# A gate input fetched three steps ahead, first in its step, with three buffers; eleven buffers for z instead of twelve

## The chip, the cores and the metric

The kernel runs on one core of one Trainium2 chip. The metric is device time in microseconds (us) of one execution, given as the median of several runs. A profiled execution is a separate one: its trace has a start and an end for each instruction of the five engines (TensorE = PE, with its weight loads shown apart as PEld; VectorE = DVE; ScalarE = ACT; GpSimd = POOL; SyncE = SP). SP does no arithmetic here. It issues nearly all transfers between the device's memory and the on-chip buffers.

## The reference, cut to what matters

Two equal layers are applied to an image x of 512 x 512 places with 64 channels. In each, x is normalised by groups of two channels over the whole image (`_gn`) and then by channels at each place (`_ln`); five products with 64 x 128 weights follow; `left` and `right` are gated; a band of nine rows of `left` is multiplied into `right`; the result is normalised over its 128 channels, multiplied by an output gate and projected back to 64 channels.

```python
xn = _ln(x, norm_scale, norm_bias)
left = (xn @ Wl + bl) * mask * jax.nn.sigmoid(xn @ Wlg + blg)
right = (xn @ Wr + br) * mask * jax.nn.sigmoid(xn @ Wrg + brg)
out_gate = jax.nn.sigmoid(xn @ Wog + bog)
out = _banded_ingoing(left, right, WIN)
out = _ln(out, out_norm_scale, out_norm_bias) * out_gate
return out @ Wo + bo
...
x = x + _L0_conv_ref(_gn(x), L0_conv_src_mask, L0_conv_norm_scale, ...)
x = x + _L1_conv_ref(_gn(x), L1_conv_src_mask, L1_conv_norm_scale, ...)
```

## The kernel before

Each layer goes over nine blocks of 64 rows (`row_blocks`), and each block in two chunks of 16 steps, so a layer has 18 chunks and 288 units of work. A unit is 64 rows by 8 columns in each half of the image (`Unit`); what leaves the layer is made in units too (`Out`). `layer` (line 784) first plans at which step each part of the work of each unit falls, and then runs a loop over steps `t` (line 846). In one step parts of several units are in hand:

- the input `z` of a unit far ahead is loaded (`load`, two transfers of 128 KB). It is scaled and moved (POOL), its statistics are taken (DVE), and one step before the unit's own step it is transposed on PE (`transposed`) and copied to `zT` by ACT (`kept`). The transposes are the last readers of the `z` buffer. `zp` (line 388) has twelve buffers. The plan lets the load run 9 to 12 steps ahead of the unit's own step, and in most of the steps of a chunk it loads one unit, in some two or none;
- `kept` also stores `zT`, the transposed input, to the device's memory under the name `later` (line 483, 256 KB), because the output gate needs it 17 or 33 steps on. `zT` has two buffers, so the copy of one unit waits for the store of the unit two before;
- `right` (line 516) is the projection of the unit from `zT`, 32 small matrix products, in two halves, "project 0" and "project 4"; ACT makes the sigmoid `sg`, and DVE the product `RO`;
- `take_left` (line 561) loads a slab `A` of the band, four transfers of 128 KB each. A chunk needs eight slabs, so they fall into a part of the steps only; `mix` ("band") multiplies with it;
- for an output unit `o`, `recall` (line 686) loads the stored `zT` back into `zg` (256 KB, pool `ztg`, line 1067, two buffers). `gates` (line 690) multiplies it with the gate's weights, in four matrix products, the only readers of `zg`; `gated` is the sigmoid of that on ACT (`gate`); `turned`, `times_gate` (DVE, `ZH`) and `end` follow; `ended` adds the residual `XR`, which `fetch` (line 739) loaded by two transfers, and stores two transfers to `mid_x` (layer 0) or to the output (layer 1).

The order of the instructions on every engine is the program's own: `InOrder` (line 373) holds each engine to the order in which the program issues, and that is why most of the profile's lines are L381, the line of that helper. Within a step the items run in the order of the lists `FIRST` and `SECOND` (lines 38 and 47). "gates" stands ahead of the projections in both, "transpose" and "keep" in the second half of the list, "end" after them in `FIRST` and just after "keep" in `SECOND`.

SP's queue in a step before the change is: loads of `z` (lines 849 to 851), two of `XR` for the next step, the slabs `A`, the load of `zg` for the step after the next (lines 856 and 857), and then, as the items come, the store of `zT` and the two stores of the output unit before. Each transfer can wait on a semaphore ahead of its issue, and what is behind it in the queue waits with it. The pools' buffers come free at run time: a load into a used buffer waits for the last reader of what was there. The load of `zg` in step `t` waits so for the gate products of step `t` itself, as there are two buffers and it loads for step `t + 2`.

Of the kernel before, what the change touches and what calls it, by code (L numbers as in the profile page):

```python
# [103 lines left out]
def tile_two_banded_layers(  # L104
# [280 lines left out]
            InOrder, (nc.tensor, nc.vector, nc.scalar, nc.gpsimd, nc.sync)  # L385
        )

    zp = ctx.enter_context(tc.tile_pool(name="zp", bufs=12))

    class Unit:  # L390

# [7 lines left out]
    def load(src: bass.AP, u: Unit):  # L399
        u.z = zp.tile([P, JU, D], F32, tag="z", name="z")  # L400
        if u.near is None:
            rows = slice(u.blk.s, u.blk.s + S)
            for e, j in enumerate((u.j, LH + u.j)):
                en.sync.dma_start(u.z[e * S : (e + 1) * S], src[rows, j : j + JU, :])
            return
        spans = [(0, u.near, u.near + JU)]
        if u.near + JU > NEAR * JQ:
            spans = [(o, u.near, u.near + JQ) for o in range(0, JU, JQ)]
        for o0, n0, n1 in spans:
            for o, r, k, m in runs(n0, n1):  # L410
                z = u.z[:, o0 + o : o0 + o + m, :].rearrange("q m c -> q (m c)")
                at, q0, q1 = r * (L + 1) + k - WIN, 0, P
                pieces = []

                if r == 0 and k < WIN:
                    q0, g = 1, min(m, WIN - k)
                    pieces = [(0, 0, g, 0), (0, g, m, at + g)]
                if r == JQ - 1 and k + m > WIN + 1:
                    q1, g = P - 1, max(0, WIN + 1 - k)
                    end = (P - 1) * JQ * (L + 1) + at  # L420
                    pieces = [(P - 1, 0, g, end), (P - 1, g, m, L * L - m)]
                en.sync.dma_start(
                    z[q0:q1],
                    strided(
                        src, (q0 * JQ * (L + 1) + at) * D, (JQ * (L + 1) * D, q1 - q0), (1, m * D)
                    ),
                )
                for q, g0, g1, a in pieces:
                    if g0 < g1:
                        en.sync.dma_start(  # L430
                            z[q : q + 1, g0 * D : g1 * D],
                            strided(src, a * D, (D, 1), (1, (g1 - g0) * D)),
                        )
# [127 lines left out]
    def take_left(n: int, h: int) -> bass.AP:  # L561


        A = lp.tile([P, HA // 2, S, 2], F32, tag="A", name="A")
        q = HA // 4
        for e in range(2):
            for s in range(2):
                en.sync.dma_start(
                    A[e * S : (e + 1) * S, s * q : (s + 1) * q].rearrange("p h i t -> p h (i t)"),
                    strided(  # L570
                        left_of, n * size + (s * H // 4 + h * q) * span + 2 * WIN,
                        (H // 2 * span, S), (span, q), (1, 2 * S),
                    ),
                )
        return A
# [110 lines left out]
    def recall(o: Out):  # L686
        o.t = ztg.tile([P, JU // 2, P], F32, tag="zg", name="zg")
        en.sync.dma_start(o.t, later[o.at])
# [95 lines left out]
    def layer(src: bass.AP, dst: bass.AP, w: dict, stats: bool, then=None):  # L784
# [4 lines left out]
        units, outs, lefts, mixes, looks, slabs = {}, {}, {}, {}, {}, {}  # L789
# [4 lines left out]
        for c in range(n_chunks):  # L794
            b, t0 = blocks[c // per], (c + 1) * NU
            for k in range(NU):
                t = c * NU + k
# [18 lines left out]
        for n in range(0, NEAR * JQ, JU):  # L816
            t = 3 + n // JU * 2
# [28 lines left out]
        for t in range(min(loads), last_t + 3):  # L846
            if then and t == max(units) + 2:
                then()
            for u in loads.get(t, []):
                if u not in early:  # L850
                    load(src, u)
            if t + 1 in outs:
                fetch(src, outs[t + 1], w, t + 1)
            for c, h in slabs.get(t, []):
                A[c, h] = take_left(c // per, h)
            if t + 2 in outs:
                recall(outs[t + 2])

            looking = []
            for o, k in looks.get(t, []):  # L860
# [26 lines left out]
            for item in order:  # L887
                name, n = item if isinstance(item, tuple) else (item, None)
# [120 lines left out]


    two = layer(mid_x, out, w, False)
    one = layer(x, mid_x, w, True, lambda: next(two))
    with tc.tile_pool(name="setup", bufs=1) as tmp:

# [49 lines left out]
    later = dram.tile([len(blocks) * LH // JU, P, JU // 2, P], F32, name="later")  # L1064

    ztp = ctx.enter_context(tc.tile_pool(name="ztp", bufs=2))
    ztg = ctx.enter_context(tc.tile_pool(name="ztg", bufs=2))
    lp = ctx.enter_context(tc.tile_pool(name="lp", bufs=NA))
    wk = ctx.enter_context(tc.tile_pool(name="wk", bufs=3))
    onp = ctx.enter_context(tc.tile_pool(name="onp", bufs=1))  # L1070
# [14 lines left out]
def build(arrays):  # L1085
    import concourse.bacc as _bacc

    nc = _bacc.Bacc("TRN2", target_bir_lowering=False, num_devices=1)
    aps = {}
    for name in _INS:  # L1090
        a = arrays[f"in_{name}_dram"]
        aps[name] = nc.dram_tensor(
            f"in_{name}_dram", a.shape, mybir.dt.from_np(a.dtype), kind="ExternalInput"
        ).ap()
    out = nc.dram_tensor("out_0_dram", aps["x"].shape, F32, kind="ExternalOutput").ap()
    layers = [{n: aps[f"L{i}_conv_{n}"] for n in _NAMES} for i in range(2)]
    with tile.TileContext(nc) as tc:  # L1097
        tile_two_banded_layers(tc, aps["x"], layers, out)
    return nc
# [10 lines left out]
```

## Time and profile before

| what | value |
|---|---|
| median of three runs | 4771.6 us (4764.16 to 4789.46) |
| the profiled execution, its time | 4769.15 us |
| the profiled execution, span from first to last instruction | 4767.2 us |
| busy share of the span: PE, PEld | 81%, 70% |
| busy share: DVE, ACT, POOL | 84%, 76%, 69% |
| mean granted TensorE clock over the span | 0.952 |
| bytes moved, mean rate | 983.48 MB, 206 GB/s |
| share of the 16 transfer engines taken by SP's queue (q1) | 74.4% |
| loads of `zg` | 576 of 256 KB |

The shares are means over stages that are unlike one another. The first 480 us or so are statistics and set-up, the first layer's output steps run from about 510 to 2540 us, the second layer's from about 2790 to 4760. An idle stretch of an engine is put down to the semaphore that ended it. "Busy" for PE means that a matrix product was in the array by a model of its end, and a busy SP is not shown at all, since all that SP does here is to wait and to issue.

### The profile page before, as it was taken

How to read it: one execution, taken by the hardware profiler on the slowest of the kernel's cores; microseconds unless marked ns; L12 is line 12 of the kernel's file. 1: busy time of each engine (PE TensorE's matmuls, PEld its weight loads, DVE VectorE, ACT ScalarE, POOL GpSimd, SP SyncE). 2: the span in 40 equal slices, each digit the busy share in tenths (PEclk: the TensorE clock that was granted, in tenths of full speed). 3: DMA queues.
4: the chain of work that ended last, by engine and by line, in shares of the span. 5: the costliest groups of instructions: out<-in, count | busy, mean ns of one | idle time of the engine just before them, and what ended most of it. 6: DMA issues, size and time to landing. Idle time of an engine off the chain costs nothing. (4 is left out here: it accounts for less than half of the span.)

```text
span 4767.2 us, 193179 instructions
## 1 busy us (share of the span) xinstructions
PE 3885.2 (81%) x76306; PEld 3337.2 (70%) x76306; DVE 4007.1 (84%) x10943; ACT 3608.6 (76%) x8410; POOL 3274.7 (69%) x3427
## 2 busy tenths in 40 slices
PE   1035899999999999999985478888888888888898
PEld 0024787888787878887864467777777777777776
DVE  7864888888888888888877488988899998999898
ACT  0023888888888888898974378888888888888887
POOL 0036888888888888888723487777777777777751
PEclk9987999999999999999997799999999999999999
DMA  7958677777777777777764867777777777777776
GB/s 311 401 120 126 182 208 204 212 217 211 212 208 208 210 208 209 214 212 210 207 171 110 104 189 208 214 220 208 210 221 214 221 212 211 213 219 215 217 200 185
DMA packets 1437809, 983.48 MB, mean 206 GB/s; under 512 B 167363, under 2 KB 1284585, under 8 KB 1432553
## 3 DMA queue, kind: packets, MB, share of 16 engines
q1 hardware_dynamic: 1432064, 969.69, 74.4%
q8 instruction: 604, 9.90, 0.9%
q14 instruction: 301, 2.46, 0.2%
q10 hardware_dynamic: 4840, 1.43, 0.1%
HBM read 658.35 MB, written 312.40 MB: 204 GB/s over the span
## 5 line engine op out<-in xcount | busy, mean ns | idle before, releaser
L381 ACT ACTIVATE on<-RO,nm,rs 128x128 f32<-128x128 f32 x3744 | 1588.5, 492 | 91.8 <-DVE nm L381 44.9
L381 PEld LDWEIGHTS banks<-pack,zT 64*128 64x128 f32 x18576 | 1304.4, 203 | 380.6 <-ACT zT L381 204.4
L381 PE MATMUL banks<-pack,zT 64*128 64x128 f32 x18576 | 1350.8, 292 | 174.4 <-ACT zT L381 149.3
L381 DVE TENSOR_TENSOR RO<-banks,sg 128x512 f32<-128x512 f32 (+1 forms) x1188 | 796.3, 677 | 464.4 <-ACT sg L381 387.6
L381 POOL TENSOR_SCALAR on<-RO,rs,nm 128x128 f32<-128x128 f32 x864 | 383.9, 451 | 975.7 <-ACT sg L381 504.5
L381 ACT ACTIVATE sg<-banks 128x512 f32<-128x512 f32 (+1 forms) x1188 | 695.0, 590 | 311.1 <-PE banks L381 287.1
L381 PE MATMUL bank<-zg,pack 64*128 64x448 f32 (+1 forms) x2304 | 727.3, 615 | 213.5 <-DMA zg<-later 193.8
L381 DVE BATCH_NORM_STATS2 sto<-RO 128x6 f32<-128x256 f32 x2304 | 803.8, 412 | 0.8
L381 DVE SCALAR_TENSOR_TENSOR ZH<-bank,pack,gate 128x448 f32<-128x448 f32 (+1 forms) x1152 | 739.5, 684 | 63.0 <-ACT gate L381 34.1
L381 ACT ACTIVATE gate<-bank 128x448 f32<-128x448 f32 (+1 forms) x1152 | 563.8, 541 | 172.6 <-issue 103.0
L381 POOL TENSOR_TENSOR z<-z,ga 128x512 f32<-128x512 f32 x536 | 681.2, 1279 | 17.2 <-DMA z<-mid_x 8.7
L381 PE MATMUL bank<-pack,ZH 128*64 128x64 f32 x18432 | 667.3, 226 | 17.8 <-DVE nm L381 16.7
L381 POOL TENSOR_TENSOR z<-z,gb 128x512 f32<-128x512 f32 x536 | 677.5, 1277 | 5.1
L381 POOL TENSOR_TENSOR z<-z,rs 128x512 f32<-128x512 f32 x586 | 618.3, 1056 | 71.6 <-DVE rs L381 44.6
L381 POOL TENSOR_TENSOR z<-z,sti 128x512 f32<-128x512 f32 x586 | 624.3, 1066 | 20.8 <-DVE sti L381 20.8
L381 PEld LDWEIGHTS bank<-pack,ZH 128*64 128x64 f32 x18432 | 587.4, 138 | 60.9 <-DVE nm L381 24.2
L381 ACT ACTIVATE zT<-banks 128x512 f32<-128x512 f32 (+1 forms) x1084 | 460.1, 475 | 72.0 <-PE banks L381 62.8
L381 DVE BATCH_NORM_STATS2 sti<-z 128x6 f32<-128x128 f32 x2344 | 504.1, 282 | 0.5 <-POOL z L381 0.3
L381 PE MATMUL bank<-ident,on 64*128 64x64 f32 x9216 | 453.8, 227 | 27.5 <-ACT gate L381 25.0
L381 PEld LDWEIGHTS bank<-zg,pack 64*128 64x128 f32 x2304 | 240.5, 191 | 336.5 <-DMA zg<-later 62.7
L381 PEld LDWEIGHTS bank<-ident,on 64*128 64x128 f32 x9216 | 426.5, 141 | 69.6 <-ACT gate L381 44.7
L381 DVE TENSOR_TENSOR XR<-bank,XR 120x512 f32<-120x512 f32 (+1 forms) x576 | 390.9, 679 | 2.5 <-PE bank L381 1.2
(154 smaller groups left out, 4020.5 us busy)
## 6 DMA issues: line engine op xcount, KB each, us to landing
later<-zT SPq DMA_DIRECT2D x576, 256.0 KB
A<-left_of SPq DMA_DIRECT2D x1152, 128.0 KB
zg<-later SPq DMA_DIRECT2D x576, 256.0 KB
z<-in_x_dram SPq DMA_DIRECT2D x576, 128.0 KB
z<-mid_x SPq DMA_DIRECT2D x576, 128.0 KB
gn_x<-in_x_dram SPq DMA_DIRECT2D x16, 4096.0 KB
XR<-in_x_dram SPq DMA_DIRECT2D x448, 112.0 KB
mid_x<-XR SPq DMA_DIRECT2D x448, 112.0 KB
```

The lines of the kernel that those rows point to most:

```text
L381: return lambda *a, **k: tc.keep_in_program_order(f(*a, **k))
```

## The change

It edits four places. `zp` has eleven buffers instead of twelve, `ztg` three instead of two; both tiles take the same room, so what is in the on-chip memory stays the same in sum. The load of `zg` in step `t` is for the output unit of step `t + 3` instead of `t + 2`, and it is issued ahead of the step's loads of `z`, `XR` and `A` instead of behind them. No transfer is added, none is removed, and the order of the instructions on PE, DVE, ACT and POOL is the same as before; on SP only the places of the `zg` loads differ. With three buffers the load in step `t` again waits for the gate products of step `t`. In the steps in which the plan loads 12 steps ahead (four of a chunk's sixteen), the load of `z` with eleven buffers waits for the transposes of the very step in which it stands; with twelve it waits for those of the step before.

```diff
-    zp = ctx.enter_context(tc.tile_pool(name="zp", bufs=12))
+    zp = ctx.enter_context(tc.tile_pool(name="zp", bufs=11))
...
         for t in range(min(loads), last_t + 3):
             if then and t == max(units) + 2:
                 then()
+            if t + 3 in outs:
+                recall(outs[t + 3])
             for u in loads.get(t, []):
                 if u not in early:
                     load(src, u)
...
             for c, h in slabs.get(t, []):
                 A[c, h] = take_left(c // per, h)
-            if t + 2 in outs:
-                recall(outs[t + 2])
...
-    ztg = ctx.enter_context(tc.tile_pool(name="ztg", bufs=2))
+    ztg = ctx.enter_context(tc.tile_pool(name="ztg", bufs=3))
```

## The prediction

> **What bounds the kernel now.** I read the windows first, for the two layers' steady stretches: span, then busy time and count of PE, PEld, DVE, ACT and POOL, the granted TensorE clock, the transfer engines' share and GB/s.
>
> ```profile
> 700.00:2300.00 1600.00, 1487.62 (x30692) 1291.98 (x30685) 1379.73 (x3753) 1418.86 (x3322) 1339.93 (x1317) 0.98 0.76 211
> 2800.00:4400.00 1600.00, 1403.50 (x27852) 1223.06 (x27854) 1446.77 (x3930) 1334.84 (x3091) 1210.82 (x1348) 0.96 0.77 214
> ```
>
> In layer 0 PE is nearest to full (93%, 112 us idle); in layer 1 DVE is (90%), PE has 196 us idle. Then the tile zg, with what its readers' engine waited for and who waited:
>
> ```profile
>   DMA zg<-later: 256.5, 131
> ...
>   PE bank L381: 193.8, 103
>   PEld bank L381: 62.7, 28
> ```
>
> PE's weight loads and products wait together, so I count the products' 193.8 us alone. The waits by engine in the two windows put 60.9 us of it into the first and 105.2 us into the second; 27.7 us are left for the edges. It is PE's largest wait in either window.
>
> Why is a load that is asked for two steps ahead late? The step is (2544.1 - 523.3) / 287 = 7.04 us in layer 0 and (4764.3 - 2806.3) / 287 = 6.82 us in layer 1 (first and last store of XR in that tile's answer). Matching the 576 loads to their products in the timeline, I find a median of 5.8 us between issue and product, not 14. The SP timeline tells why (start, duration, engine, what):
>
> ```profile
> 3573.27 1.22 SPq L381 DMA_DIRECT2D z<-mid_x  x2
> 3574.54 2.07 SPq L381 DMA_DIRECT2D XR<-mid_x  x2
> 3576.71 2.58 SPq L381 DMA_DIRECT2D A<-left_of  x4
> 3579.39 0.55 SPq L381 DMA_DIRECT2D zg<-later  x1
> 3580.04 0.55 SPq L381 DMA_DIRECT2D later<-zT  x1
> ...
> 3593.85 0.45 SPq L381 DMA_DIRECT2D zg<-later  x1
> 3598.06 0.52 SPq L381 DMA_DIRECT2D later<-zT  x1
> ```
>
> SP issues one thing after another, about 0.6 us each, and is a step behind PE in the steps with slabs A. The product of the zg load at 3579.39 then stood idle for it:
>
> ```profile
> 3578.31 0.46 PE L381 MATMUL banks<-ident,z 64*128 64x64 f32 x8
> 3582.64 1.87 PE L381 MATMUL bank<-zg,pack 64*128 64x448 f32 x4 [3.86 <-DMA zg<-later]
> 3584.29 3.63 PE L381 MATMUL banks<-pack,zT 64*128 64x128 f32 x32
> ```
>
> So a load lands about 3.25 us after its issue (3582.64 - 3579.39), and the array then runs slowly: the 32 products took 3.63 us, against 1.95 us one step before (3574.82). The windows say the same, with the granted clock third from the right:
>
> ```profile
> 3575.00:3580.00 5.00, 3.77 (x88) 3.50 (x86) 5.00 (x15) 4.76 (x12) 3.79 (x6) 1.00 0.61 172
> 3582.60:3588.00 5.40, 5.37 (x42) 4.56 (x44) 1.38 (x4) 1.61 (x4) 0.00 (x0) 0.50 0.83 243
> ```
>
> **The change, part by part.** *The load's lead.* It gains one step (6.8 to 7.0 us) and what it passes in its own step: two z at 0.587 us, two XR at 0.46 to 0.48 us, up to four A at 0.615 us (medians of the tiles' SP rows), so 1 to 4.6 us. The latest loads leave PE idle 3.9 to 4.6 us. 8 us more than cover that even if SP falls 3 us further behind: I take all 193.8 us as removed.
>
> *The slow clock.* A clock of 0.98 and 0.96 in the two windows is (1 - 0.98) x 2 x 1600 = 64 us and 128 us at half speed. Laid beside the timeline, about 48 us of the one and 85 us of the other begin within some 7 us after a zg wait, and 17 us at the edges: 150 us, half of it lost, 75 us. PE so loses 194 + 75 = 269 us to zg. In the trace I find slow products after zg waits from 2 us up (32 products at 415 ns each, against 272 ns).
>
> The Trainium skill, "TensorE: Matmul & The Clock Gate", section "HAM oscillation — how this bites in real kernels", puts the fall of the clock at idle gaps over about 3.4 us. By that rule only the waits of that length, 11 of them, would have slow products behind them, one stretch of 3.4 us each, and the term would be an estimated 19 us instead of 75. The rows show it from 2 us, so 75 stays.
>
> *What of it comes off the end.* In layer 0, PE is the bound, and DVE's waits (192.5 us for sg in the window) follow from PE: of 60.9 + 24 = 85 us I take 0.85, 72 us. In layer 1, folding the waits by step number mod 16, a fifth falls on steps in which DVE has no idle time at all and brings nothing; of the rest I take three quarters, since DVE is busy 90% and PE already waits 61.8 us for its RO. Of 105.2 + 43 = 148 us that is 0.6, 89 us. At the edges 27.7 + 8 = 36 us, 0.7 of it, 25 us. Sum 186 us. The bounds are 0 (all passed on) and 269 (all of it).
>
> *Which queue is next to be late.* SP's work does not shrink. Per step: two z 1.17, two XR 0.92 to 0.96, two A on the mean 1.23, zg 0.46, store of zT 0.55, two stores 0.96 to 1.01, ten issues with some 0.08 us between them: 6.2 us of 7.04 and 6.82. A slab step with four z has 14 issues, 9 us; a step without z and A has six, 3.5 us. SP falls behind through two thirds of a chunk and catches up in its last steps; there it waits for ACT, as at 3593.85, where it had 3.7 us to spare (3598.06 less 3594.30). The waits of SP's queue in layer 1's window:
>
> ```profile
> SPq L381 <- ACT zT L381: 71.4, 42, 4.0
> ```
>
> That is about 5 us a chunk (114 us, 14 to the window), and with its shorter waits some 9 us: this is what a faster PE can take before SP sets the pace. A faster PE leaves SP further behind at the end of the slab steps, by as much as PE gains until then: some 6 us in layer 1, 4 us in layer 0. What has least slack is the store of zT, which frees the buffer for the copy two units later. It is issued right behind zg's old place. At 3571.41 plus 3.25 us it lands at 3574.7, and ACT writes at 3579.00: 4.3 us of slack. z in layer 1 has 2 to 4 us before POOL scales it, on an engine that waits 301 us for sg in that window. XR and A have 7 us and more, but in layer 0 XR has only 3.5 us before POOL adds the bias. I charge 1.5 us a chunk in layer 1 and 0.5 us in layer 0, 14 chunks each: 28 us; bounds 0 and 6 us a chunk, at which the gain is gone.
>
> *The wait at the head of a step.* zg's load waits for the step's gate products, now ahead of z, XR and A. Before, zg was issued 3.5 us after those products began, in the earliest step of a chunk, with two XR (1 us) in front; the products take 1.0 to 1.25 us. SP so comes to the head more than 1 us after they are done: nothing, at worst 1 us in the three steps where SP is in time anyway.
>
> *Eleven buffers for z.* Four loads of a chunk now wait for the transposes of the same step. Matching loads with the transposes of the unit eleven before, three of the four are already issued 1 to 7 us after them, the last at about -0.6 us, -3.8 us at worst. Behind it wait XR, the store of zT and the two output stores. 0.6 us x 36 chunks = 22 us of SP's time, most of it from its spare: 4 us; bounds 0 and, with 3.8 us for each of the four, 15 us a chunk.
>
> Sum: 186 - 28 - 4 = 154 us off. The profiled span 4767.2 becomes 4613; the median shown is 4.4 us above that span, so **4618 us**.
>
> [...]
>
> **The rivals.** *The wait is passed on.* SP stays where it is, PE waits for zT or DVE for RO instead; for it speak 6.2 us of issue in 6.8 us and DVE's 90%; against it, that SP has idle time in each chunk's last steps and that DVE idles 3.7 us behind the very wait shown above. It gives 4750 to 4790 us. *Everything comes off*, 269 us: 4771.6 - 269 = 4503 us; against it, DVE in layer 1 is then full. *Slower:* the z loads. If PE runs ahead less than I think, or SP less far behind, each of the four loads waits up to 3.8 us with XR, A and the stores behind it, 15 us a chunk. SP's work, 16 x 6.2 + 4 = 103 us with the chunk's uneven waits, would become 118 us against chunks of 113 and 109 us: 5 to 9 us a chunk, 36 of them, 250 us at worst, with half of it 4900 us. It decides from some 10 us a chunk on. Against it: the rows above, and that a faster PE makes these transposes earlier, not later. *It does not do what it says* (the load still lands late since SP is two steps behind) is part of the first.
>
> **How the numbers follow.** Forecast and near it (4550 to 4740) 0.70, everything off (below 4550) 0.07, passed on 0.11, slower 0.12. A measurement of this kernel can tell about 0.5%, 24 us, from no change. Faster 0.78, same 0.10, slower 0.12. The range is 4550 to 4770.
>
> **What would show it.** In the trace after: no zg in PE's waits; the clock near 0.99 in layer 0; DVE's wait for sg at half; SP's wait for ACT's zT shorter; issue to product of zg over 10 us. It is wrong if PE waits for zT as long as for zg now, if SP's queue shows PE's transposes as its longest wait, or if steps without a zg wait got longer.

## The result, and the profile after

| | kernel before | changed kernel |
|---|---|---|
| median of four runs | 4772.93 us | 4633.11 us |
| lowest and highest | 4764.16, 4789.46 us | 4627.84, 4647.15 us |
| span of the profiled execution | 4767.2 us | 4644.6 us |
| mean granted TensorE clock | 0.952 | 0.959 |

The changed kernel is faster: ratio 0.972, 95% interval 0.9688 to 0.9752, 140 us less. The profiled execution of the changed kernel is the slowest of its four, so its span shows 123 us of that.

The wait that the forecast was about is gone. This is what the tile zg answers in the changed kernel (who waited for it: us, times):

```profile
who waited for it (us, times):
  ACT zT L381: 3.6, 3
  ACT gate L381: 2.7, 5
```

PE, which had waited 193.8 us for it, isn't in the list. The windows of 1600 us in the two layers, with the columns as before (span, busy of PE, PEld, DVE, ACT, POOL, granted clock, transfer share, GB/s):

```profile
700.00:2300.00 1600.00, 1541.97 (x32205) 1341.30 (x32203) 1440.81 (x3915) 1478.78 (x3477) 1392.89 (x1369) 1.00 0.80 220
...
2700.00:4300.00 1600.00, 1445.66 (x28724) 1254.06 (x28722) 1494.39 (x4085) 1371.90 (x3178) 1269.40 (x1401) 0.97 0.81 221
```

In layer 0 more instructions fit into the window (PE 32205 for 30692), PE is busy 96% of it and the clock stays at 1.00. In layer 1 the clock only went from 0.96 to 0.97, and PE still has 154 us idle. The waits by engine in that second window say why (us, times, longest):

```profile
POOL z L381 <- DMA z<-mid_x: 151.2, 45, 5.8
...
PE banks L381 <- ACT zT L381: 66.8, 71, 3.3
...
ACT zT L381 <- DMA later<-zT: 53.7, 38, 3.1
```

and, of SP's own queue in the same window:

```profile
SPq L381 <- ACT zT L381: 19.3, 20, 4.9
```

PE's wait for zT was 12.9 us in as long a window before. ACT can't write zT because the store that frees the buffer lands late. SP's own wait for ACT, 71.4 us before, is down to 19.3: SP has hardly any time left in which it waits for work: the pauses of 0.3 us or more between two of its issues, added up from the trace, are 85 us in the layer 1 window of the kernel before and 30 us in this one. One place shows the chain in full, here by PE, ACT and SP:

```profile
3491.67 2.06 PE L381 MATMUL banks<-pack,zT 64*128 64x128 f32 x32 [0.49 <-ACT zT L381]
...
3495.53 1.04 PE L381 MATMUL bank<-zg,pack 64*128 64x448 f32 x4
3499.34 3.79 PE L381 MATMUL banks<-pack,zT 64*128 64x128 f32 x32 [2.77 <-ACT zT L381]
```

```profile
3498.42 0.87 ACT L381 ACTIVATE zT<-banks 128x512 f32<-128x512 f32 x2 [2.36 <-DMA later<-zT]
```

```profile
3490.40 0.88 SPq L381 DMA_DIRECT2D XR<-mid_x  x2
3491.32 2.82 SPq L381 DMA_DIRECT2D A<-left_of  x4
3494.24 1.24 SPq L381 DMA_DIRECT2D later<-zT  x1
3495.58 1.04 SPq L381 DMA_DIRECT2D out_dram<-XR  x2
3496.71 0.40 SPq L381 DMA_DIRECT2D zg<-later  x1
```

The gate products at 3495.53 find their zg in time. The store issued at 3494.24, behind four transfers of A, lands some 4 us later, ACT writes at 3498.42, and PE's projections start after an idle 2.77 us, at half speed (3.79 us instead of the 2.06 of the step before): the same picture as before the change with another tile in zg's place.

The sections of the two profiled executions, from the first and last gate products of each layer in the timeline:

| section | before | after | difference |
|---|---|---|---|
| start to the first gate product | 510.2 | 527.6 | +17.4 |
| layer 0, first to last gate product | 2027.4 | 1942.2 | -85.2 |
| from there to layer 1's first gate product | 255.9 | 277.2 | +21.3 |
| layer 1, first to last gate product | 1964.9 | 1888.3 | -76.6 |
| rest | 8.9 | 9.2 | +0.3 |

The layers gained 162 us, and the two sections in which a layer fills its stages (the "fills" below) lost 39 us. A chunk of 16 steps, as the mean of the 14 that follow each layer's first, went from 116.6 and 114.0 us to 111.4 and 109.6.

### The profile page after: what moved, and what is told of

Same layout as the page of the kernel before. It is cut to its first block, busy times and chain, and to the rows that moved or that the text cites. A ratio compares the mean times of both kernels' runs of the same rounds, so it can differ in the third digit from the quotient of the medians.

```text
span 4644.6 us, 192669 instructions
## 1 busy us (share of the span) xinstructions
PE 3860.9 (83%) x76306; PEld 3310.7 (71%) x76306; DVE 3999.6 (86%) x10943; ACT 3596.2 (77%) x8410; POOL 3278.3 (71%) x3427
## 5 line engine op out<-in xcount | busy, mean ns | idle before, releaser
L381 PEld LDWEIGHTS banks<-pack,zT 64*128 64x128 f32 x18576 | 1270.1, 197 | 467.4 <-ACT zT L381 324.5
L381 PE MATMUL banks<-pack,zT 64*128 64x128 f32 x18576 | 1326.1, 287 | 262.2 <-ACT zT L381 234.8
L381 PEld LDWEIGHTS bank<-pack,ZH 128*64 128x64 f32 x18432 | 589.6, 139 | 64.6 <-DVE nm L381 27.5
L381 PE MATMUL banks<-ident,z 64*128 64x64 f32 x4336 | 251.1, 234 | 131.2 <-DVE RO L381 68.7
```

The costliest lines, as they stand in the source:

```text
L381: return lambda *a, **k: tc.keep_in_program_order(f(*a, **k))
```

## The experiments

Seven kernels were run, in two groups. Each group had its own runs of the kernel before beside it, with medians of 4794.87 us for the first four and 4762.75 us for the last three, so ratios to these are compared and not times. In each text that was put down ahead of a run, "own theory" is what was expected and "rival" is the other reading.

**Eleven buffers for z, alone.**

```diff
-    zp = ctx.enter_context(tc.tile_pool(name="zp", bufs=12))
+    zp = ctx.enter_context(tc.tile_pool(name="zp", bufs=11))
```

> The kernel before with eleven buffers for z and nothing else changed. Own theory: the two fills of the layers, which became longer in the changed kernel (first gate product at 527.6 us instead of 510.2, and 277 instead of 256 us between the layers' output steps), are the price of the twelfth z buffer; so the fills are longer here too, the waits for zg stay near 190 us, and the time is 4795 to 4820 us. Rival: the fills are longer because zg's load stands first in its step and holds up the z loads; then this kernel is the same as before, 4773 us within 0.5%, with its first gate product near 510 us.

Ratio 1.0119 (1.0097 to 1.0141), 4853.63 us: 1.2% slower, a little more than was expected. PE's waits for zg stayed, as expected (205.3 us). The first gate product comes at 544.2 us and the section between the layers takes 286 us, against 521.8 and 265 us in the kernel below that was run beside it and has twelve buffers (the place alone): together some 44 of the 59 us. SP's waits while layer 0 fills (180 to 560 us here) name the place:

```profile
SPq L381 <- PE bank L381: 47.6, 7, 13.0
```

In the kernel before (180 to 520 us) that line was

```profile
SPq L381 <- PE bank L381: 9.6, 5, 4.5
```

and in the changed kernel (180 to 540 us)

```profile
SPq L381 <- PE bank L381: 46.5, 8, 13.0
```

The SP timeline of the kernel with eleven buffers shows which transfers wait:

```profile
321.43 0.56 SPq L381 DMA_DIRECT2D later<-zT  x1
327.52 1.11 SPq L381 DMA_DIRECT2D z<-in_x_dram  x2
328.74 0.56 SPq L381 DMA_DIRECT2D later<-zT  x1
337.33 1.11 SPq L381 DMA_DIRECT2D z<-in_x_dram  x2
```

SP is ready at 322.0 and 329.3 and can issue the loads of z only 5.5 and 8 us later. In the fill SP is ahead of PE and all buffers are taken; a load of z that waits for the transposes of an earlier unit (the instructions that ended these waits in the trace) holds up everything behind it. So the longer fills come from the missing buffer and not from zg's place: here zg's load is where it was. Chunks were 117.3 and 114.8 us, 0.7 to 0.8 above the kernel before in its own profiled execution, though these two come from different groups.

**The lead alone, and the place alone.** The first has the load three steps ahead with three buffers and eleven for z, but behind z, XR and A; the second has it first in the step, two steps ahead, with two buffers and twelve for z.

The first, against the kernel before (its lines of the two pools are those of the change and are left out here):

```diff
             for c, h in slabs.get(t, []):
                 A[c, h] = take_left(c // per, h)
-            if t + 2 in outs:
-                recall(outs[t + 2])
+            if t + 3 in outs:
+                recall(outs[t + 3])
```

> The changed kernel with zg's load back behind z, XR and A in its step, still three steps ahead with three buffers, and z with eleven. Own theory: the step of lead does it, the place in the step adds little: PE waits under 20 us for zg, and the time is within 0.7% of the changed kernel's 4633 us. Rival: the place in the step is what counts; then over 100 us of zg waits stay and the time is over 4700 us.

Ratio 0.9762 (0.9734 to 0.979), 4676.85 us. PE's wait for zg fell to 43.3 us, not under 20. The ratio is 0.4% from the changed kernel's and the intervals overlap, so the lead by itself, with the buffers that it takes, does most of the change.

The second:

> The kernel before with zg's load first in its step, still two steps ahead with two buffers, and z with twelve. Own theory: the load gains only the 1 to 4.6 us of the issues that it passes, so some third of the wait stays, 30 to 90 us, and the time is 4680 to 4740 us. Rival (the place is enough, and the third buffer and the lead are not needed): the wait goes to under 20 us and the time is at or below 4633 us, below it by the two fills' some 38 us if those are z's.

```diff
         for t in range(min(loads), last_t + 3):
...
+            if t + 2 in outs:
+                recall(outs[t + 2])
             for u in loads.get(t, []):
...
-            if t + 2 in outs:
-                recall(outs[t + 2])
```

Ratio 0.970 (0.9673 to 0.9727), 4647.04 us. Both expectations missed. The rival named the time (by its ratio no worse than the changed kernel) and not the wait. The wait stayed, even above the 30 to 90 us of my theory, and the time was better than in it:

```profile
  DMA zg<-later: 149.4, 88
...
  PE bank L381: 102.0, 60
  PEld bank L381: 47.4, 28
```

PE waits 102 us for zg and layer 1's chunk is 109.9 us, against 109.6 in the changed kernel, in which PE doesn't wait for zg at all, and 110.1 with the lead alone. SP's wait for ACT's zT in 1600 us of layer 1 (2750 to 4350) is 13 to 19 us in all three, and its pauses of 0.3 us or more add up to 16 to 24 us. So there is a floor of about 110 us under layer 1's chunk, and which tile PE waits for at that floor makes no difference. The next kernels test whether the floor is SP's issuing.

**Fewer issues after the change.** The same bytes of A go in two transfers instead of four, 16 issues fewer of some 160 in a chunk.

```diff
         for e in range(2):
-            for s in range(2):
-                en.sync.dma_start(
-                    A[e * S : (e + 1) * S, s * q : (s + 1) * q].rearrange("p h i t -> p h (i t)"),
-                    strided(
-                        left_of, n * size + (s * H // 4 + h * q) * span + 2 * WIN,
-                        (H // 2 * span, S), (span, q), (1, 2 * S),
-                    ),
-                )
+            en.sync.dma_start(
+                A[e * S : (e + 1) * S].rearrange("p (s h) i t -> p s h (i t)", s=2),
+                strided(
+                    left_of, n * size + h * q * span + 2 * WIN,
+                    (H // 2 * span, S), (H // 4 * span, 2), (span, q), (1, 2 * S),
+                ),
+            )
```

> The changed kernel with each slab A loaded by two transfers of 256 KB instead of four of 128 KB; the same bytes, 16 issues of some 160 fewer in a chunk, about 10 us of SyncE's time. Own theory: after the change SyncE's issuing is late in layer 1 and makes the new waits (PE for zT whose buffer the store frees late, GpSimd for z); then these waits shrink from some 67 and 151 us in 1600 us to under half, layer 1's chunk falls from 109 us towards 106, layer 0's by about 1, and the time is 4550 to 4605 us. Rival: DVE and PE set the pace and SyncE's lateness costs nothing; then 4620 to 4645 us, whatever the waits do.

Ratio 0.959 (0.9569 to 0.9611), 4598.06 us. Chunks are 110.2 and 105.9 us. In 1600 us of layer 1 (2750 to 4350) the wait of PE that had come with the change is small again (it was 64.4 us), POOL's wait for z is down to 6.6 us from 151, and SP waits for ACT:

```profile
SPq L381 <- ACT zT L381: 77.5, 46, 5.0
```

```profile
PE banks L381 <- ACT zT L381: 11.2, 31, 1.3
```

SP's pauses of 0.3 us or more are 126 us here. PE's largest wait is now for POOL (85.1 us for the tile `on`, the normalised result), while DVE is busy 97% of the window.

**Fewer issues without the change.** The same edit of A on the kernel before.

> The kernel before with each slab A loaded by two transfers of 256 KB instead of four of 128 KB, zg's load and the buffers untouched. Own theory (zg was late because SyncE's issuing was late, not because of its own lead or place): 16 issues fewer in a chunk, some 10 us, bring SyncE back to less than a step behind, the wait for zg falls from 194 to under 40 us without zg being touched, and the ratio to the kernel before is 0.955 to 0.97. Rival (zg needs its lead or its place): most of the wait stays, and the ratio is over 0.98.

Ratio 0.9555 (0.9533 to 0.9578), 4548.76 us. The tile zg now shows

```profile
who waited for it (us, times):
  PE bank L381: 28.8, 28
  PEld bank L381: 17.4, 14
```

instead of 193.8 and 62.7, though neither zg's load nor a buffer was touched: own theory held. This is a larger gain than that of the change under study, and the fills are as short as before (508.0 and 253 us).

**The place and fewer issues together**, with two buffers for zg and twelve for z.

> The kernel before with zg's load first in its step, two steps ahead and two buffers, twelve for z, and slabs A in two transfers. Own theory: no wait for zg (under 10 us), fills as short as before, layer 1's chunk near 105.7 us and layer 0's near 110 as in the changed kernel with two transfers for A; the ratio to the kernel before is 0.945 to 0.955, some 40 us below the changed kernel with the same A. Rival (the third buffer and the third step are needed once SyncE is in time): waits for zg over 50 us stay and the ratio is 0.96 or over.

Ratio 0.951 (0.9488 to 0.9532), 4527.45 us, the fastest of all. PE waits once, 1.4 us, for zg. Chunks are 110.2 and 105.9 us, as in the changed kernel with the same A, and the fills are as short as in the kernel before (first gate product at 507.8 us, 253 us between the layers). The windows show what is left:

```profile
700.00:2300.00 1600.00, 1551.06 (x32429) 1352.89 (x32429) 1455.08 (x3953) 1494.28 (x3512) 1387.56 (x1368) 1.00 0.84 221
2800.00:4300.00 1500.00, 1403.80 (x28151) 1222.54 (x28149) 1455.56 (x3968) 1343.06 (x3124) 1225.60 (x1363) 0.99 0.89 231
```

PE is busy 97% in layer 0 (1551.06 of 1600), DVE 97% in layer 1 (1455.56 of 1500).

**More issues after the change.** zg's load cut into two of 128 KB, 16 issues more in a chunk.

```diff
-        en.sync.dma_start(o.t, later[o.at])
+        q = JU // 4
+        for k in range(0, JU // 2, q):
+            en.sync.dma_start(o.t[:, k : k + q], later[o.at][:, k : k + q])
```

> The changed kernel with zg's load cut into two transfers of 128 KB, the same bytes and 16 issues more in a chunk. Own theory (SyncE's issuing sets layer 1's pace after the change): SyncE's work of some 105 us a chunk becomes some 114, layer 1's chunk goes from 109 to 115 us or over and layer 0's from 111 to 115 or over, the ratio to the kernel before is 1.00 to 1.03. Rival (SyncE is late, but another engine sets the pace): the ratio stays under 0.98.

Ratio 1.0183 (1.0155 to 1.0211), 4846.28 us. Chunks are 118.0 and 116.5 us: 6.6 and 6.9 us more than the changed kernel for 16 issues more. ACT's wait for the store of zT shows the same victim; it was 212.9 us in the whole run of the changed kernel, and 129.0 us in 1600 us of layer 1 here are against 53.7 there:

```profile
ACT zT L381 <- DMA later<-zT: 384.9, 130, 16.1
```

PE doesn't wait for zg here either; the kernel loses all that the change had brought and more. SP's pauses of 0.3 us or more in 1600 us of layer 1 are 10 us. A chunk of layer 1 so takes 105.9, 109.6 and 116.5 us with about 144, 160 and 176 issues, with the order of the transfers unchanged; at 105.9 us it is DVE that is full, not SP.

A rival is that the cut load makes smaller packets and that the transfer engines are what slows down. The share of the 16 transfer engines taken by SP's queue (packets, MB, share of the span) speaks against it, first in the changed kernel and then here:

```profile
q1 hardware_dynamic: 1432064, 969.69, 77.1%
```

```profile
q1 hardware_dynamic: 1515008, 969.73, 72.8%
```

There are 6% more packets, but the engines were taken for no longer (some 3520 us of the whole run, against 3580). With A in two transfers after the change the share is higher, 82.5%, and the kernel faster.

## Why the prediction held, and where it did not

The forecast was 4618 us and the measured median 4633 us, inside the range, 140 us gained for 154 forecast.

- *The load's lead removes zg's wait*: right, 193.8 us to none. What I did not see is that either of its two parts is nearly enough: the place, which I had taken as an addition of 1 to 4.6 us, gives the same ratio with two buffers for zg and twelve for z, in part because it doesn't pay for longer fills.
- *The slow clock, 75 us*: the right mechanism, over-sized as a net gain. Stretches at half clock from 510 us on went from 361 to 275 us, so 43 us of PE's time came back. In layer 0's window 58 us of them became 3.4. In layer 1's window 85 us were left of 126, and about half of these (44 us, begun within 5 us after one) follow the new waits for zT, as at 3499.34. So the stretches behind zg's waits went about as counted, and the new waits brought others.
- *What comes off the end and which queue is late next*: 186 less 28, 158 us, against 162 us measured between the first and last gate products of the layers. That the two are so close is in part luck: I cut layer 1's gain to 0.6 because of DVE, but what held its chunk at 109.6 us was SP's queue. With 16 issues fewer the same change takes it from 114.0 to 105.9 us, 8.1 us instead of 4.4. The store of zT behind zg's old place was named as having the least slack, and it is what PE now waits for. Its size was a partial miss: PE's wait for zT grew by 54 us in layer 1's window, where I charged 21 for all of SP's lateness there, and POOL waits 151 us for z, on an engine that had the time.
- *SP's floor, 6.2 us a step*: low. The three orders of the same 160 issues end near 110 us a chunk of layer 1, 6.9 us a step, and two kernels moved that with the number of issues alone. I had counted no issue that takes longer than its median: in the changed kernel's layer 1 window the issues took 1416 us, while their medians add up to 1266; why some take longer is not shown. The step itself was taken too short, since 7.04 and 6.82 us are means with the short last chunks in them (99.7 and 82.5 us between gate products); by the chunks of 116.6 and 114.0 us it was 7.3 and 7.1. So SP was not a limit still some way off in layer 1, it is what the change ran into.
- *The wait at the head of a step costs nothing*: SP's waits for PE's bank in layer 0's window fell from 43.1 to 27.5 us; no cost shows.
- *Eleven buffers for z, 4 us*: this is the term that failed. I worked it out for the chunks, in which SP is behind PE, and not for the two fills, where it is ahead and every buffer is taken. It measured 39 us in the fills of the changed kernel, and 1.2% alone. A sign of being wrong that I had named, PE's transposes as the longest wait of SP's queue, is what the fills show (46.5 us in the first).
- *Passed on* was a rival at 0.11. In layer 1 it was half true: a new wait of the same kind and the same slow clock behind it stand in zg's place, only smaller (66.8 us for zT where there were 105.2 for zg).

The Trainium skill's rule in "DMA: Bandwidth & Descriptors", section "Rules for kernel authors", that many small transfers should be joined into one large one, gives 64 KB as the size under which overhead rules. Here it paid at 128 KB: the issue of A took SP 615 ns (median) for 128 KB and 637 ns for 256 KB, so half the issues took half the time, and the limit in the changed kernel's layer 1 was the issuing queue rather than the transfer engines (0.81 busy there, and 0.89 in the fastest kernel's layer 1). The rule in "TensorE: Matmul & The Clock Gate", section "HAM oscillation — how this bites in real kernels", names idle gaps over about 3.4 us; in the changed kernel the clock fell after 2.77 us. In the kernel before it did so behind many shorter waits, but not all: of the 30 waits of PE for zg between 2 and 3.4 us, 22 had slow products behind them (over 300 ns each as the mean of the next 32, against 272).

```profile
3490.00:3495.60 5.60, 5.11 (x98) 4.25 (x95) 5.60 (x16) 5.27 (x14) 5.52 (x9) 1.00 0.90 217
3499.30:3505.90 6.60, 6.56 (x88) 6.37 (x89) 2.82 (x7) 4.48 (x10) 2.98 (x4) 0.54 0.88 217
```

The granted clock, third from the right, is 0.54 after that gap and 1.00 before it.

Left open: three buffers for zg together with twelve for z were not tried, and the clock's share was not isolated by a kernel of its own.

## What to carry to other kernels

When a prefetched tile is late, look at the queue that issues it before giving it more lead: if the queue issues without a pause while the reader waits, count its issues and join transfers first. Moving one load forward gained 2.8% here, until the queue itself set the pace; from there on it only chooses who waits. A buffer taken from a deep prefetch is to be priced where the pipeline fills too: here the queue ran ahead in the fills, and each wait for a buffer stopped all that was behind it.

## What the runs showed of the hardware that was not expected

SP's time for an issue hardly depended on the bytes: for A 615 ns at 128 KB and 637 ns at 256 KB, for zg 462 ns at 256 KB and 424 ns at 128 KB (medians). One engine's queue so became the bound of layer 1 in a kernel whose four computing engines were each busy 79 to 93% of that window, and 16 issues of 160 were worth 3 to 6% of a chunk of layer 1.
